# Last output projection with tokens on partitions, its residual turned in squares of 32 during the last layer's attention

## The chip, the cores and the metric

The kernel runs on one core of a Trainium2 chip. The metric is the device time of one execution in microseconds (us): the median over three runs for the kernel before. Beside the timed runs there is one execution taken by the hardware profiler; it has its own time, and its span runs from the first to the last instruction recorded. The core's engines are TensorE (PE in the profile, with its weight loads as PEld), VectorE (DVE), ScalarE (ACT), GpSimd (POOL) and SyncE (SP). Each takes its own instructions in the order in which the program lists them. SP and POOL issue the transfers (DMAs) here; sixteen DMA engines carry them out. The tensors that carry data between stages lie in the chip's memory (DRAM below); tiles lie in the core's own memory, 128 partitions wide.

## What is computed

The input is an image of 48 x 48 tokens with 768 channels. Two layers follow, each a group norm, a multi-head attention with relative positions, and a residual:

```python
def _L1_conv_ref(x, qkv_w, qkv_b, proj_w, proj_b, rel_pos_h, rel_pos_w):
    ...
    qkv = x.reshape(B, N, C) @ qkv_w.T + qkv_b
    ...
    attn = jnp.einsum('bnd,bmd->bnm', q * scale, k)
    ...
    attn = (attn.reshape(B * nh, H, W, H, W) + rel_h[:, :, :, :, None] + rel_w[:, :, :, None, :]).reshape(B * nh, N, N)
    attn = jax.nn.softmax(attn, axis=-1)
    out = jnp.einsum('bnm,bmd->bnd', attn, v)
    ...
    out = out @ proj_w.T + proj_b
    return out
...
x = x + _L0_conv_ref(_gn(x), ...)
x = x + _L1_conv_ref(_gn(x), ...)
return x
```

N is 2304 tokens, C 768 channels, 12 heads of 64 channels. The first layer differs in its weights only (a low-rank addition to q and v). The change concerns the last line of the last layer: `x + (out @ proj_w.T + proj_b)`, with x the residual.

## The kernel before

**Layout.** Through both layers the activations lie with channels on partitions: a block of 384 tokens (QB) is a tile of 128 partitions, 6 channel tiles (CT) and 384 tokens. There are six such blocks (NQB), in three pairs (b, b + 3). The input is turned into this layout at the start by TensorE transposes; the residual of the second layer is kept in DRAM in the same layout (`residuals[1]`, six tensors f_res1_b).

**Stages.** For each layer: group norm, projection to k, v and q with the relative-position terms, attention, output projection. The order of each engine's instructions is set by a scheduler when the program is built, from the order of the source; instructions wrapped in `in_order` keep their order in the source on their engine.

**Attention** (`attend_plain`, L864). It works through 30 blocks: 6 pairs of heads, and for each of them the queries in four blocks of 512 and one of 256. Numbered from 0, blocks 4, 9, 14, 19, 24 and 29 are the short ones. For each block the scores are made in two batches of nine key tiles (ps_sc, three buffers, L967), ScalarE takes the exponential (pt, L981), VectorE adds the pt up (sum, L987) and TensorE multiplies them by the values (ps_ov, L1006); the values of a batch follow the scores of the next. At a block's end the sum is cast in three parts (L996 to L999), TensorE sums it over the keys (ps_d), VectorE takes the reciprocal (L1021) and scales the result (L1025); POOL stores rec and o (L1030, L1032).

What the attention loads comes through SP's queue: the queries and the rel rows of the next block (`fetch_queries`, two q and 24 rel loads; two sets of buffers), and during the last block of a pair of heads the keys and values of the next pair (`keys_of`, L893, and `values_of`, L906; one set of buffers, so that a load waits until the old keys have been read).

After each block from block 1 on, the loop takes one step of the generator `beside` (L1080, L1081):

```python
                if i > 0:
                    next(beside, None)
```

In the kernel before, `beside` (L1249) first loads the projection's weights `w_all` and bias `bt`, and then takes four steps on VectorE that prepare the factors of the seven products.

**Output projection** (`out_project`, L1123). A 2 x 2 block product is made by seven products in place of eight (`seven_products`, L433). For each of the three pairs of token blocks and each of three channel tiles (`co`) there are seven products psy of three matmuls each: weights as the stationary side, 128 output channels on the partitions of the result, 384 tokens along it. ScalarE copies two of the products out (kept_p), VectorE forms the sums and adds them, with the bias, into y, which holds the residual (L1183, L1184). In the last layer y must then be turned to tokens on partitions: 36 TensorE transposes for a pair of blocks (psn, L1200), six copies by ScalarE (L1202) and six stores to the output on SP (L1203). The tiles for the first pair of blocks (y_1_0, y_1_1, oT_1_0, oT_1_1) lie where attention's buffers come free (L1265), and are loaded before the attention ends. `judge` (L1084) looks at all reciprocals and decides whether a second, slower variant of the whole computation must run; it doesn't run with these inputs.

Of the kernel before, what the change touches and what calls it, by code (L numbers as in the profile page):

```python
# [9 lines left out]
F32 = mybir.dt.float32  # L10
# [8 lines left out]
P = 128  # L19
# [52 lines left out]
def compute(ctx: ExitStack, tc: tile.TileContext, x, layers, out, run, bad):  # L72
# [1011 lines left out]
    def judge(ps_j):  # L1084

        cols = NH * N // P
        with tc.tile_pool(name="judge", bufs=1) as jp:
            r = jp.tile([P, 2, cols], F32, tag="r", name="judged")
            low = jp.tile([P, 2, cols], F32, tag="low", name="low")
            good = jp.tile([P, 2], F32, tag="good", name="good")  # L1090
            col = jp.tile([P, 1], F32, tag="col", name="col")
            nc.vector.memset(col, 1.0)
            for li in range(2):
                nc.sync.dma_start(
                    r[:, li, :],
                    recs[li].rearrange("h q -> (h q)").rearrange("(p c) -> p c", p=P),
                )
# [5 lines left out]
            ps = ps_j.tile([P, 1024], F32, tag="n", name="n_good")[0:1, 0:2]  # L1103
# [16 lines left out]
            )  # L1120
            lo += n

    def out_project(ly, li, od, w, bt, first, res, xT, next_res, beside):  # L1123


        last = xT is None
        with ExitStack() as es:
            tp = es.enter_context(tc.tile_pool(name="p3_t", bufs=1, **REUSE))
            kp = es.enter_context(tc.tile_pool(name="p3_k", bufs=2, **REUSE))
            rp = es.enter_context(tc.tile_pool(name="p3_r", bufs=2, **REUSE))  # L1130
            yp = es.enter_context(tc.tile_pool(name="p3_y", bufs=2, **REUSE))
            ps_y = es.enter_context(tc.tile_pool(
                name="ps_y", bufs=4 if last else 8, space=PSUM, **REUSE
            ))
            ps_n = None
            if last:
                op = es.enter_context(tc.tile_pool(name="p3_o", bufs=2 * TPB, **REUSE))
                ps_n = es.enter_context(tc.tile_pool(name="ps_n", bufs=2, space=PSUM, **REUSE))
            for at, b in enumerate((1, 0, 2)):
                pair = (b, b + HB)  # L1140
                if last and not shifted and at == HB - 1:
                    judge(ps_n)
                if not last:
                    y = [xT[i] for i in pair]
                elif at == 0:
                    y = first[2:]
                else:
                    y = yp.tile([P, 2, CT, QB], F32, tag="y", name=f"y_{b}")
                    y = [y[:, i] for i in range(2)]
# [12 lines left out]
                blocks = {  # L1162
                    f"{i + 1}{j + 1}": oT[j][:, i * HP : (i + 1) * HP]
                    for i in range(2) for j in range(2)
                }
                t = tp.tile([P, 4, HP, QB], F32, tag="t", name=f"oT_t_{b}")
                right = sums_of_b(blocks, t)
                for co in range(HP):
                    def product(i):
                        left_of, right_of = FACTORS[i]  # L1170
                        ps = ps_y.tile([P, QB], F32, tag="y", name=f"psy_{b}_{co}_{i}")
                        for t in range(HP):
                            nc.tensor.matmul(  # L1173
                                ps, lhsT=w[left_of][:, t, ts(co, P)], rhs=right[right_of][:, t, :],
                                start=(t == 0), stop=(t == HP - 1),
                            )
                        return ps

                    def result(at, x, more):
                        i, j = int(at[0]) - 1, int(at[1]) - 1  # L1180
                        ch = i * HP + co
                        to = y[j][:, ch, :]
                        nc.vector.tensor_add(to, to, more)  # L1183
                        nc.vector.scalar_tensor_tensor(  # L1184
                            to, x, bt[:, ch : ch + 1], to, ALU.add, ALU.add
                        )
                        if not last:
                            nc.vector.bn_stats(stats[:, ch, pair[j], :], to)
# [4 lines left out]
                for i in range(2):  # L1193
                    if not last:
                        nc.gpsimd.dma_start(next_res[pair[i]], y[i])
                        continue
                    for j in range(TPB):
                        ps = ps_n.tile([P, 1024], F32, tag="n", name=f"psn_{b}_{i}_{j}")
                        for t in range(CT):
                            nc.tensor.transpose(ps[:, ts(t, P)], y[i][:, t, ts(j, P)], ident)  # L1200
                        o = op.tile([P, C], F32, tag="o", name=f"o_{b}_{i}_{j}")
                        nc.scalar.copy(o, ps[:, 0:C])  # L1202
                        nc.sync.dma_start(out[ts(pair[i] * TPB + j, P), :], o)  # L1203

    residuals = [[scratch(f"res{li}_{b}", [P, CT, QB]) for b in range(NQB)] for li in range(2)]
    def begin(li, es):
# [14 lines left out]
    for li, ly in enumerate(layers):  # L1221
# [19 lines left out]
            scratch(f"o{li}_{lo}", [CT, P, min(OB, N - lo)]) for lo in range(0, N, OB)  # L1241
        ]
        with tc.tile_pool(name="p3_w", bufs=1, **REUSE) as p3:
            w_all = p3.tile([P, CT, C], F32, tag="w", name="wproj")
            bt = p3.tile([P, CT], F32, tag="bt", name="bproj")
            s = p3.tile([P, 3, HP, HP * P], F32, tag="s", name="wproj_s")
            w, steps = sums_of_a(matrix_blocks(w_all, HP * P), *(s[:, i] for i in range(3)))
# [12 lines left out]
            if last:  # L1260
                p3_first = es.enter_context(
                    tc.tile_pool(name="p3_first", bufs=1, side="right", **REUSE)
                )

                y_late, *first_out, y_soon = (  # L1265
                    p3_first.tile([P, CT, QB], F32, tag=name, name=name)
                    for name in ("y_1_1", "oT_1_0", "oT_1_1", "y_1_0")
                )
                first_out += [y_soon, y_late]
# [12 lines left out]

            k_steps = prepare()
            out_project(
                ly, li, od, w, bt, first_out, residuals[li], xT,
                None if last else residuals[li + 1], iter(()) if last else k_steps,
            )
            if not last:
# [57 lines left out]
```

## Time and profile before

| what | us |
|---|---|
| median of 3 runs | 3268.39 |
| lowest, highest | 3266.74, 3270.97 |
| the profiled execution | 3271.64 |
| its span | 3269.8 |
| last layer's attention, in the span | about 2107 to 3126 |
| last output projection, in the span | 3126 to 3270 |

The mean TensorE clock granted in the profiled execution is 0.993 of full speed. All times inside the execution below are us from the start of the span. A line of the timeline gives the start, the length, the engine, the source line, the operation, the tiles written and read, their shapes and a count; in brackets stands the idle time before it and what ended that. "SPq" is SP's queue issuing transfers. In a line of groups, the number after the bar is the busy time and the mean in ns of one instruction. In the list of transfers the last number is the median time from issue to landing. In the row of a stretch there is, for each engine, the busy time and the number of instructions, then the clock, the share of the DMA engines' time and GB/s.

Of the last output projection the profile shows 378 records of psy matmuls (two for each of the 189 matmuls), 486 ns each on the average, overlapping in steady work: 12 records in 3.87 us. The 108 transposes take 14.0 us of busy time in all, the 18 copies 801 ns each.

### The profile page before, as it was taken

To read this page: it belongs to the slowest core of one execution; us is meant where nothing else is said; L and a number is where in the kernel's file an instruction comes from. 1 tells how busy PE (TensorE), PEld (TensorE's weight loads), DVE (VectorE), ACT (ScalarE), POOL (GpSimd) and SP (SyncE) were. 2 spreads that over 40 slices of the span, in tenths; PEclk is the share of its full clock that TensorE was granted. 3 is DMA by queue.
4 is the path that set the end of the run, shared out by engine and by line. 5 is a ranking of instruction groups with operands and counts; after the bars stand their busy time and mean duration, and the time that the engine had idled before them with its cause. 6 is when DMAs were issued, how large, how long until landed. Compare 5 with 4: busy or idle time off the path is not lost.

```text
span 3269.8 us, 50021 instructions
## 1 busy us (share of the span) xinstructions
PE 3219.1 (98%) x19708; PEld 2010.7 (61%) x19708; DVE 2098.2 (64%) x2275; ACT 1446.6 (44%) x1655; POOL 374.0 (11%) x701
## 2 busy tenths in 40 slices
PE   8999999999999999999989999999999999999998
PEld 5555666565666565665555566656666665656665
DVE  8432437777777777777775234577777777777764
ACT  3111436555555565553011014555555565656511
POOL 2145110000000000000012531100000000000000
PEclk9999999999999999999999999999999999999999
DMA  7333388353626262634234335865444363525251
GB/s 266 128 85 74 127 263 213 77 131 77 139 68 152 65 154 64 145 71 159 102 121 147 61 105 185 250 151 119 94 115 101 99 120 79 140 75 129 55 196 60
DMA packets 219091, 405.61 MB, mean 124 GB/s; under 512 B 41392, under 2 KB 108880, under 8 KB 215008
## 3 DMA queue, kind: packets, MB, share of 16 engines
q1 hardware_dynamic: 177984, 260.08, 32.4%
q0 software_dynamic: 40864, 142.23, 13.8%
q8 instruction: 159, 2.61, 0.3%
q14 instruction: 84, 0.69, 0.1%
HBM read 253.27 MB, written 148.89 MB: 123 GB/s over the span
## 4 chain that ended last, share of the span: by engine, by line
PE 88%; issue 6%; DVE 2%; DMA 1%; POOL 1%; SPq 1%; ACT 1%; POOLq 0%; DVEq 0%
PE ps_sc L954 34%; PE ps_ov L954 25%; PE ps_v L523 7%; PE psy L1173 7%; PE ps_q L698 6%; PE ps_k L523 4%; PE ps_d L954 1%; PE psr L637 1%; DMA f_r<-relw 1%; POOL f_k L567 1%; PE psc L637 0%; DVE relw L392 0%; PE psn L1200 0%; ACT relw L391 0%; DMA flat<-in_relh_t_dram 0%
## 5 line engine op out<-in xcount | busy, mean ns | idle before, releaser
L987 DVE TENSOR_TENSOR sum<-sum,pt 128x1024 f32<-128x1024 f32 (+1 forms) x960 | 1070.8, 1115 | 188.3 <-ACT pt L981 97.2
L981 ACT ACTIVATE pt<-ps_sc 128x1024 f32<-128x1024 f32 (+1 forms) x1080 | 1011.2, 941 | 192.1 <-PE ps_sc L954 105.8
L954 PE MATMUL ps_sc<-q,k 64*128 64x512 f32 (+1 forms) x8640 | 1086.1, 371 | 1.3 <-DVE relw L392 0.6
L954 PEld LDWEIGHTS ps_sc<-q,k 64*128 64x128 f32 x8640 | 786.6, 186 | 208.1 <-issue 43.9
L954 PE MATMUL ps_ov<-pt,v 128*64 128x512 f32 (+1 forms) x4320 | 857.7, 551 | 0.0
L954 PEld LDWEIGHTS ps_ov<-pt,v 128*64 128x64 f32 x4320 | 301.1, 137 | 497.6 <-issue 443.0
L954 PE MATMUL ps_sc<-rel,places 64*128 64x512 f32 (+1 forms) x2160 | 415.3, 371 | 2.9 <-DMA rel<-f_r 2.9
L698 PE MATMUL ps_q<-xT,w_q 128*128 128x384 f32 x864 | 285.7, 489 | 0.6 <-DVE v L587 0.6
L1032 POOL DMA_DIRECT2D f_rec<-rec x120 | 58.3, 490 | 1776.6 <-DVE rec L1021 1776.4
L1026 ACT ACTIVATE o<-o,v_bias 128x512 f32<-128x512 f32 (+1 forms) x60 | 40.9, 682 | 449.5 <-DVE o L1025 449.5
L954 PEld LDWEIGHTS ps_sc<-rel,places 64*128 64x128 f32 x2160 | 213.3, 185 | 33.2 <-DMA rel<-f_r 2.9
L698 PEld LDWEIGHTS ps_q<-xT,w_q 128*128 128x128 f32 x864 | 163.4, 191 | 110.3 <-issue 2.9
L1021 DVE RECIPROCAL rec<-ps_d 128x512 f32<-128x512 f32 (+1 forms) x60 | 181.8, 3030 | 2.5 <-PE ps_d L954 2.5
L987 DVE TENSOR_TENSOR sum<-pt 128x1024 f32<-128x1024 f32 (+1 forms) x60 | 67.1, 1119 | 140.2 <-ACT pt L981 140.2
L601 POOL DMA_DIRECT2D f_v<-v x288 | 137.3, 485 | 105.8 <-DVE v L587 94.4
L704 DVE TENSOR_SCALAR x_q<-ps_q,bt 128x384 f32<-128x384 f32 x72 | 44.3, 617 | 160.0 <-PE ps_q L698 160.0
L523 PE MATMUL ps_k<-xt,w_k 128*128 128x384 f32 x432 | 143.4, 488 | 3.5 <-DVE xt L427 2.6
L996 ACT CAST sum<-sum 128x1024 bf16<-128x1024 f32 (+1 forms) x60 | 57.6, 960 | 167.7 <-DVE sum L987 167.7
L523 PE MATMUL ps_k<-xT,w_k 128*128 128x384 f32 x324 | 116.4, 513 | 4.7 <-DVE xT L249 4.6
L523 PEld LDWEIGHTS ps_k<-xt,w_k 128*128 128x128 f32 x432 | 81.6, 190 | 62.9 <-PE ps_k L523 3.0
L999 DVE TENSOR_TENSOR sum<-sum,sum 128x1024 bf16<-128x1024 f32 (+1 forms) x60 | 67.1, 1119 | 61.6 <-ACT sum L998 61.6
L997 DVE TENSOR_TENSOR sum<-sum,sum 128x1024 f32<-128x1024 f32 (+1 forms) x60 | 67.1, 1118 | 61.5 <-ACT sum L996 61.5
(172 smaller groups left out, 2383.4 us busy)
## 6 DMA issues: line engine op xcount, KB each, us to landing
rel<-f_r SPq DMA_DIRECT2D x1152, 96.0 KB, 4.3
f_k<-xs POOLq DMA_DIRECT2D x72, 384.0 KB, 2.9
f_q<-xs_q POOLq DMA_DIRECT2D x48, 576.0 KB, 3.8
k<-f_k SPq DMA_DIRECT2D x48, 576.0 KB, 4.9
q<-f_q SPq DMA_DIRECT2D x96, 256.0 KB, 3.3
f_r<-relh POOLq DMA_DIRECT2D x48, 432.0 KB, 5.0
f_r<-relw POOLq DMA_DIRECT2D x8, 2592.0 KB, 18.2
f_v<-v POOLq DMA_DIRECT2D x288, 48.0 KB, 2.0
```

The lines of the kernel that those rows point to most:

```text
L523: nc.tensor.matmul(ps, lhsT=x, rhs=y, start=(t == 0), stop=(t == HP - 1))
L601: nc.gpsimd.dma_start(vd[to : to + KG, :], v[ts(r, KG), k])
L698: nc.tensor.matmul(ps, lhsT=w[:, t, ts(pr, P)], rhs=xT[b][:, t, :], start=(t == 0), stop=(t == CT - 1),)
L954: in_order(nc.tensor.matmul(*args, **kwargs))
L981: nc.scalar.activation(pt, ps[:, :, 0 : self.n], AF.Exp)
L987: nc.vector.tensor_add(self.sum, self.first if kt == 1 else self.sum, pt)
L996: nc.scalar.copy(hi, self.sum)
L997: nc.vector.tensor_sub(self.sum, self.sum, hi)
L999: nc.vector.tensor_sub(lo, self.sum, mid)
L1021: nc.vector.reciprocal(self.rec, ps)
L1032: nc.gpsimd.dma_start(recs[li][2 * self.pair + r : 2 * self.pair + r + 1, to], self.rec[r * HD : r * HD + 1, :],)
L1173: nc.tensor.matmul(ps, lhsT=w[left_of][:, t, ts(co, P)], rhs=right[right_of][:, t, :], start=(t == 0), stop=(t == HP - 1),)
```

## The change

In the last layer's output projection the two sides of each matmul change places: the attention's output is the stationary side, 128 tokens at a time, and the weights' factors stream through, 384 channels. The result has tokens on partitions, as the output wants it, so the transposes and the copies behind them are gone, and the sums are stored straight from y. The residual must then also lie with tokens on partitions, and carry the bias, which is no longer one number per partition.

That is done by the new generator `turn`, run in the steps of `beside` during the last layer's attention, for each of the six blocks of 384 tokens: load the block of the residual, add the bias in six activations on ScalarE, transpose it in squares of 32 by one VectorE instruction over 128 x 2304 elements, and store it in 24 transfers on POOL, each of 32 partitions by 12 runs of 32 numbers, to `res_tokens` in DRAM, tokens by channels. The tile `both` holds a block and its transposed form; it has one buffer, with the tag "w" that the projection's weights use after it. The output projection loads its y from `res_tokens`.

```diff
-    def out_project(ly, li, od, w, bt, first, res, xT, next_res, beside):
+    def out_project(li, od, w, bt, first, res, xT, next_res, beside):
...
-            yp = es.enter_context(tc.tile_pool(name="p3_y", bufs=2, **REUSE))
+            yp = es.enter_context(tc.tile_pool(name="p3_y", bufs=2 * TPB, **REUSE))
             ps_y = es.enter_context(tc.tile_pool(
-                name="ps_y", bufs=4 if last else 8, space=PSUM, **REUSE
+                name="ps_y", bufs=7 if last else 8, space=PSUM, **REUSE
             ))
...
-                for i in range(2):
-                    nc.sync.dma_start(y[i], res[pair[i]])
+                if last:
+                    def tokens(x, j):
+                        return x.rearrange("(k b j p) c -> b j p k c", k=2, b=HB, j=TPB)[b, j]
+
+                    for j in range(TPB):
+                        nc.sync.dma_start(y[j], tokens(res, j))
...
-                for co in range(HP):
+                for part in range(HP):
...
+                            x, y = w[left_of][:, t], right[right_of][:, t]
+                            if last:
+                                x, y = y[:, ts(part, P)], x
+                            else:
+                                x = x[:, ts(part, P)]
                             nc.tensor.matmul(
-                                ps, lhsT=w[left_of][:, t, ts(co, P)], rhs=right[right_of][:, t, :],
-                                start=(t == 0), stop=(t == HP - 1),
+                                ps, lhsT=x, rhs=y, start=(t == 0), stop=(t == HP - 1)
                             )
...
+                        if last:
+                            to = y[part][:, j, ts(i, HP * P)]
+                            nc.vector.tensor_add(to, to, more)
+                            nc.vector.tensor_add(to, to, x)
+                            return
...
                     seven_products(kp, QB, product, result)
+                    if last:
+                        for k in (1, 0):
+                            nc.sync.dma_start(tokens(out, part)[:, k], y[part][:, k])
...
-                    for j in range(TPB):
-                        ps = ps_n.tile([P, 1024], F32, tag="n", name=f"psn_{b}_{i}_{j}")
-                        for t in range(CT):
-                            nc.tensor.transpose(ps[:, ts(t, P)], y[i][:, t, ts(j, P)], ident)
-                        o = op.tile([P, C], F32, tag="o", name=f"o_{b}_{i}_{j}")
-                        nc.scalar.copy(o, ps[:, 0:C])
-                        nc.sync.dma_start(out[ts(pair[i] * TPB + j, P), :], o)
+    def turn(res, to, pool, bt):
+        for b in range(NQB):
+            both = pool.tile([P, 2, CT, QB], F32, tag="w", name=f"x_turned_{b}")
+            x, turned = both[:, 0], both[:, 1]
+            in_order(nc.sync.dma_start(x, res[b]))
+            yield
+            for t in range(CT):
+                in_order(nc.scalar.activation(
+                    x[:, t], x[:, t], AF.Identity, bias=bt[:, t : t + 1]
+                ))
+                if t == HP - 1:
+                    yield
+            in_order(nc.vector.transpose(
+                turned.rearrange("p t q -> p (t q)"), x.rearrange("p t q -> p (t q)")
+            ))
+            rows = to[ts(b, QB), :].rearrange("(f i) c -> i f c", i=32)
+            for t in range(CT):
+                for r in range(P // 32):
+                    lo = t * P + r * 32
+                    in_order(nc.gpsimd.dma_start(
+                        rows[:, :, lo : lo + 32],
+                        turned[ts(r, 32), t].rearrange("p (f j) -> p f j", j=32),
+                    ))
...
-            def beside(w_all=w_all, bt=bt, steps=steps, ly=ly):
+            def beside(li=li, ly=ly, p3=p3, bt=bt, w=w):
+                in_order(nc.sync.dma_start(bt, ly.proj_bt))
+                if li == 1:
+                    yield from turn(residuals[1], res_tokens, p3, bt)
+                w_all = p3.tile([P, CT, C], F32, tag="w", name="wproj")
+                s = p3.tile([P, 3, HP, HP * P], F32, tag="s", name="wproj_s")
                 in_order(nc.sync.dma_start(w_all, ly.proj_w.rearrange("(t p) n -> p t n", p=P)))
-                in_order(nc.sync.dma_start(bt, ly.proj_bt))
+                factors, steps = sums_of_a(
+                    matrix_blocks(w_all, HP * P), *(s[:, i] for i in range(3))
+                )
+                w.update(factors)
                 yield
                 yield from steps
```

The tiles of the first pair of blocks are laid out anew for y's new shape (y_1_0, y_1_1, y_1_2, each 128 tokens of both blocks by 768 channels; as much memory in all as before), and judge's one matmul gets a small accumulator of its own in place of a buffer of the transposes.

More of the change, by code (lines that the diff above doesn't have):

```diff
@@ L1102, in judge @@
                 )
-            ps = ps_j.tile([P, 1024], F32, tag="n", name="n_good")[0:1, 0:2]
+            ps = ps_j.tile([P, 2], F32, tag="n", name="n_good")[0:1]
             nc.tensor.matmul(ps, lhsT=col, rhs=good, start=True, stop=True)
@@ L1130, in out_project @@
             rp = es.enter_context(tc.tile_pool(name="p3_r", bufs=2, **REUSE))
-            yp = es.enter_context(tc.tile_pool(name="p3_y", bufs=2, **REUSE))
+            yp = es.enter_context(tc.tile_pool(name="p3_y", bufs=2 * TPB, **REUSE))
             ps_y = es.enter_context(tc.tile_pool(
-                name="ps_y", bufs=4 if last else 8, space=PSUM, **REUSE
+                name="ps_y", bufs=7 if last else 8, space=PSUM, **REUSE
             ))
-            ps_n = None
+            ps_j = None
             if last:
-                op = es.enter_context(tc.tile_pool(name="p3_o", bufs=2 * TPB, **REUSE))
-                ps_n = es.enter_context(tc.tile_pool(name="ps_n", bufs=2, space=PSUM, **REUSE))
+                ps_j = es.enter_context(tc.tile_pool(name="ps_j", bufs=1, space=PSUM, **REUSE))
             for at, b in enumerate((1, 0, 2)):
@@ L1141, in out_project @@
                 if last and not shifted and at == HB - 1:
-                    judge(ps_n)
+                    judge(ps_j)
                 if not last:
@@ L1147, in out_project @@
                 else:
-                    y = yp.tile([P, 2, CT, QB], F32, tag="y", name=f"y_{b}")
-                    y = [y[:, i] for i in range(2)]
+                    y = [
+                        yp.tile([P, 2, C], F32, tag="y", name=f"y_{b}_{j}") for j in range(TPB)
+                    ]
                 if at == 0:
@@ L1156, in out_project @@
                     fetch_output(oT[i], od, pair[i])
-                for i in range(2):
-                    nc.sync.dma_start(y[i], res[pair[i]])
+                if last:
[4 more added lines that the diff above has]
+                else:
+                    for i in range(2):
+                        nc.sync.dma_start(y[i], res[pair[i]])
                 if at == 0:
@@ L1167, in out_project @@
                 right = sums_of_b(blocks, t)
-                for co in range(HP):
+                for part in range(HP):
                     def product(i):
                         left_of, right_of = FACTORS[i]
-                        ps = ps_y.tile([P, QB], F32, tag="y", name=f"psy_{b}_{co}_{i}")
+                        ps = ps_y.tile([P, QB], F32, tag="y", name=f"psy_{b}_{part}_{i}")
                         for t in range(HP):
+                            x, y = w[left_of][:, t], right[right_of][:, t]
+                            if last:
+                                x, y = y[:, ts(part, P)], x
+                            else:
+                                x = x[:, ts(part, P)]
                             nc.tensor.matmul(
-                                ps, lhsT=w[left_of][:, t, ts(co, P)], rhs=right[right_of][:, t, :],
-                                start=(t == 0), stop=(t == HP - 1),
+                                ps, lhsT=x, rhs=y, start=(t == 0), stop=(t == HP - 1)
                             )
@@ L1180, in result @@
                         i, j = int(at[0]) - 1, int(at[1]) - 1
-                        ch = i * HP + co
+                        if last:
[3 more added lines that the diff above has]
+                            return
+                        ch = i * HP + part
                         to = y[j][:, ch, :]
@@ L1186, in result @@
                         )
-                        if not last:
-                            nc.vector.bn_stats(stats[:, ch, pair[j], :], to)
+                        nc.vector.bn_stats(stats[:, ch, pair[j], :], to)
                     seven_products(kp, QB, product, result)
+                    if last:
+                        for k in (1, 0):
+                            nc.sync.dma_start(tokens(out, part)[:, k], y[part][:, k])
                 for _ in beside:
                     pass
-                for i in range(2):
-                    if not last:
+                if not last:
+                    for i in range(2):
@@ L1195, in out_project @@
                         nc.gpsimd.dma_start(next_res[pair[i]], y[i])
-                        continue
-                    for j in range(TPB):
-                        ps = ps_n.tile([P, 1024], F32, tag="n", name=f"psn_{b}_{i}_{j}")
-                        for t in range(CT):
-                            nc.tensor.transpose(ps[:, ts(t, P)], y[i][:, t, ts(j, P)], ident)
-                        o = op.tile([P, C], F32, tag="o", name=f"o_{b}_{i}_{j}")
-                        nc.scalar.copy(o, ps[:, 0:C])
-                        nc.sync.dma_start(out[ts(pair[i] * TPB + j, P), :], o)
+    def turn(res, to, pool, bt):
[21 more added lines that the diff above has]
+                    ))
@@ L1205, in compute @@
     residuals = [[scratch(f"res{li}_{b}", [P, CT, QB]) for b in range(NQB)] for li in range(2)]
+    res_tokens = scratch("res_tokens", [N, C])
     def begin(li, es):
@@ L1243, in compute @@
         with tc.tile_pool(name="p3_w", bufs=1, **REUSE) as p3:
-            w_all = p3.tile([P, CT, C], F32, tag="w", name="wproj")
             bt = p3.tile([P, CT], F32, tag="bt", name="bproj")
-            s = p3.tile([P, 3, HP, HP * P], F32, tag="s", name="wproj_s")
-            w, steps = sums_of_a(matrix_blocks(w_all, HP * P), *(s[:, i] for i in range(3)))
-            def beside(w_all=w_all, bt=bt, steps=steps, ly=ly):
+            w = {}
+            def beside(li=li, ly=ly, p3=p3, bt=bt, w=w):
[4 more added lines that the diff above has]
+                s = p3.tile([P, 3, HP, HP * P], F32, tag="s", name="wproj_s")
                 in_order(nc.sync.dma_start(w_all, ly.proj_w.rearrange("(t p) n -> p t n", p=P)))
-                in_order(nc.sync.dma_start(bt, ly.proj_bt))
+                factors, steps = sums_of_a(
+                    matrix_blocks(w_all, HP * P), *(s[:, i] for i in range(3))
+                )
+                w.update(factors)
                 yield
@@ L1263, in compute @@
                 )
-                y_late, *first_out, y_soon = (
-                    p3_first.tile([P, CT, QB], F32, tag=name, name=name)
-                    for name in ("y_1_1", "oT_1_0", "oT_1_1", "y_1_0")
+                y_2, y_1, *first_out, y_0 = (
+                    p3_first.tile(shape, F32, tag=name, name=name)
+                    for name, shape in (
+                        ("y_1_2", [P, 2, C]), ("y_1_1", [P, 2, C]), ("oT_1_0", [P, CT, QB]),
+                        ("oT_1_1", [P, CT, QB]), ("y_1_0", [P, 2, C]),
+                    )
                 )
-                first_out += [y_soon, y_late]
+                first_out += [y_0, y_1, y_2]
             else:
@@ L1284, in compute @@
             out_project(
-                ly, li, od, w, bt, first_out, residuals[li], xT,
+                li, od, w, bt, first_out, res_tokens if last else residuals[li], xT,
                 None if last else residuals[li + 1], iter(()) if last else k_steps,
```

## The prediction

> **What bounds the kernel now.** I read the page's busy table first, then the busy time by stretches, then the last layer's attention and the end of the span in order of time.
>
> ```profile
> PE 3219.1 (98%) x19708; PEld 2010.7 (61%) x19708; DVE 2098.2 (64%) x2275; ACT 1446.6 (44%) x1655; POOL 374.0 (11%) x701
> ...
> core 0: us, PE busy (x) PEld busy (x) DVE busy (x) ACT busy (x) POOL busy (x), PEclk, DMA share, GB/s
> 2107.00:3126.00 1019.00, 1017.60 (x7735) 638.56 (x7732) 745.24 (x636) 583.08 (x631) 45.98 (x89) 1.00 0.47 110
> ```
>
> TensorE is busy 98% of the span. The second row is the last layer's attention, 2107 to 3126 us: TensorE works 1017.6 of 1019.0 us there, VectorE 745 (73%), ScalarE 583 (57%). So nothing added on the last two engines costs time unless TensorE is made to wait; the same holds for a queue.
>
> TensorE waits if keys are late. The keys of the next pair of heads have one set of buffers (L896), so they are fetched in the last block of a pair. The first such change in this layer, SP's queue and then TensorE:
>
> ```profile
> 2254.60 1.01 SPq L946 DMA_DIRECT2D rel<-f_r  x1
> 2255.71 13.92 SPq L899 DMA_DIRECT2D k<-f_k  x4
> 2273.24 0.37 SPq L908 DMA_DIRECT2D v<-f_v  x1
> ...
> 2269.09 4.11 PE L954 MATMUL ps_ov<-pt,v 128*64 128x256 f32 x36
> 2273.12 1.19 PE L954 MATMUL ps_sc<-q,k 64*128 64x512 f32 x8
> ```
>
> SP takes its instructions in order. It issues the first two key loads at 2255.7, once the old keys are read (the row's 13.92 us reach to the last two, which wait for the second half). A key load lands 4.9 us after issue, at 2260.6, and the first score of the next pair starts at 2273.12: 12.5 us in hand.
>
> The end of the span:
>
> ```profile
> 3256.82 0.61 DVE L1184 SCALAR_TENSOR_TENSOR y<-psy,bproj,y 128x384 f32<-128x384 f32 x1
> 3257.48 0.20 PEld L1200 LDWEIGHTS psn<-ident,y 128*128 128x128 f32 x2 [0.42 <-DVE y L1184]
> 3257.85 1.50 ACT L1202 COPY o<-psn 128x768 f32<-128x768 f32 x2 [6.89 <-PE psn L1200]
> ...
> 3260.46 1.58 PE L1200 MATMUL psn<-ident,y 128*128 128x128 f32 x12 [0.19 <-ACT o L1202]
> 3261.37 1.50 ACT L1202 COPY o<-psn 128x768 f32<-128x768 f32 x2 [0.26 <-PE psn L1200]
> ```
>
> VectorE has the last sum at 3257.43; 36 transposes and six copies follow, and the last copy ends at 3262.87. Only then can the last store go.
>
> **What is removed.** 108 transposes (psn, L1200) and 18 copies (L1202). In the steady stretch 12 matmul records of psy take 3.87 us. After the first group of blocks TensorE needs 7.81 us from the first transpose (weights at 3166.25) to the first record of the third product (3174.06); the 12 psy records among them are worth 3.87, so the transposes cost 3.94. After the second, 3210.83 to 3218.96: 8.13 - 3.87 - 0.12 for judge's matmul, which stays, = 4.14. At the end 3262.87 - 3257.43 = 5.44. **Sum 13.5 us off the path.** The swapped operands leave 189 products of 128x128 by 128x384; the value products (ps_v, L523) run that way round already at 486 ns a record, and psy's records take 486. I cost the swap at nothing. The bias add in place (scalar_tensor_tensor, 615 ns) becomes an add (555 ns), 36 times: 2.2 us of an engine with idle time here. Stores now leave per 128 tokens and not after a whole group: 384 KB each, as before. Seven product buffers for four only help.
>
> **What is moved into the last attention.** For each of six blocks of 384 tokens: one load of 1152 KB on SP, six activations of 128x384, one VectorE transpose of 128x2304, 24 stores on POOL of 48 KB, each 384 runs of 128 bytes; 6, 36, 6 and 144 in all. `next(beside)` is called once after each block from the second on, and two calls make one block of x: block 1 loads x 0, block 2 does three activations, block 3 the other three, the transpose, the 24 stores, **and the load of x 1, which goes into the same buffer and so waits until all 24 stores have landed**. That pattern repeats every second block; after block 13 the projection's weights take the buffer the same way.
>
> The wait stands in SP's queue. Behind it stands what SP issues next. In the changed program's instruction order these are: for x 1, twelve rel loads and then the keys of pair 1; for the weights, eight rel loads and then the keys of pair 3. Blocks 3 and 13 are both followed by the short last block of a pair (256 queries). For x 2 to x 5 the waits fall into long blocks and only queries and rel rows needed a block later stand behind.
>
> Durations for the first, in the clock of this trace (block 3's sums end at about 2250):
>
> ```profile
> 2247.78 1.04 ACT L998 CAST sum<-sum 128x1024 bf16<-128x1024 f32 x1 [1.29 <-DVE sum L997]
> 2249.95 5.40 ACT L981 ACTIVATE pt<-ps_sc 128x512 f32<-128x512 f32 x9 [1.14 <-PE ps_sc L954]
> ...
> 2250.00 1.35 DVE L412 TENSOR_TENSOR wproj_s<-wproj_s,wproj 128x1152 f32<-128x1152 f32 x1
> ...
> L1026 ACT ACTIVATE o<-o,v_bias 128x512 f32<-128x512 f32 (+1 forms) x60 | 40.9, 682 | 449.5 <-DVE o L1025 449.5
> ...
> L630 POOL DMA_DIRECT2D f_q<-xs_q x48 | 34.6, 723 | 203.3 <-ACT xs_q L386 176.2 <-DVE xs_q L387 17.0 <-ACT columns L714 10.1
> L601 POOL DMA_DIRECT2D f_v<-v x288 | 137.3, 485 | 105.8 <-DVE v L587 94.4
> f_v<-v POOLq DMA_DIRECT2D x288, 48.0 KB, 2.0
> ```
>
> - Three activations: between 0.510 (128x256, same line) and 0.725 us (128x512), so 0.62 each, 1.85 us from the end of the cast at 2248.82: 2250.7. The next block's exponentials start 0.7 us later than 2249.95; three score buffers of 1.15 us each hide that.
> - The transpose has no row. The 128x1152 add above takes 1.35 us, so 128x2304 takes 2.7 at the same rate; bounds 1.35 (twice that rate) and 5.4 (half of it). I take 2.7: 2253.4. VectorE's own delay is hidden: it idles 2.4 us before 2263.
> - The stores: POOL's time per store runs from 0.485 us (16 rows, f_v) to 0.723 (384 rows, f_q, the same number of pieces). I take 0.723: 24 x 0.723 = 17.4; bounds 11.6 and, with the 0.88 us of the 768-piece fu load, 21. The last lands 2.0 us later (f_v; bounds 1.5 and 5). **SP goes on at 2253.4 + 17.4 + 2.0 = 2272.8**, where it was at 2248 before.
> - Then x 1 (0.4 us), twelve rel loads at 0.62 us each as in this stretch (2252.75, 2253.36, ...): 7.4, and the keys at 2280.6. They land 4.9 us later, 2285.5, or 2.9 later still if the 1152 KB ahead of them move at some 400 GB/s, as the key loads do in the DMA row of this stretch. I take 2286. TensorE wanted them at 2273.1: **13 us of standing still.** With the low bounds (transpose 1.35, stores 11.6, landing 1.5) SP goes on at 2265.2 and the keys land at 2278: 5. With the high ones, 2282.2 and 2298: 25.
> - The weights after block 13: eight rel loads (5.0) but 2304 KB ahead of the keys (5.8 at 400 GB/s): keys at 2272.8 + 0.4 + 5.0 + 5.8 + 4.9 = 2288.9 in the same clock, 2283.1 if the weights don't hold them up. I take 2287: **14 us** (bounds 2 and 25, by the same ends).
> - For x 2 to x 5, SP goes on about 23 us into a block of 37.5 and x lands 9.9 us after (the y load of the same size): 33. ScalarE meets x at the block's end, so 4 us are left, and I cost these at nothing. With the high bounds x lands at 43 and each costs 3 us after the buffers: 12 in all.
>
> The rest of POOL's queue, the f_rec and f_o stores behind the 24, is up to 9 us late; its readers come blocks later.
>
> Do 128-byte rows go slower than the queue issues them? The f_rec stores are such rows:
>
> ```profile
> q0 software_dynamic: 64, 0.00, 1.6%
> f_rec<-rec POOLq DMA_DIRECT2D x2, 2.0 KB, 1.5
> ```
>
> Those are 2.5 us in which two stores ran: 64 packets, 1.6% of 16 x 2.5 us, 10 ns each. At 10 ns the 24 packets that one store gives each DMA engine take 0.24 us, a third of the 0.72 of their issue. [...] The f_v row above (one every 0.485 us, each 2.0 us to landing) shows that stores overlap; what thousands of short writes cost together, no row here shows.
>
> **Sum.** -13.5 + 13 + 14 = +13.5 us on the profiled execution (3271.6 us, of which 3269.8 are span): 3285. Against the median of the runs, 3268.4, which is 3.2 lower: **3282 us**, slower by 0.4%.
>
> **Rivals.** About 0.2% (6.5 us) is what this kernel's runs can tell from no change.
> 1. *The wait is covered: faster.* Place: SP's queue after blocks 3 and 13. Price 0 for 27: 3255 us. Keys come in time if SP goes on by 2260, that is if the 24 stores are out within 5 us, 0.2 us each; it decides for "faster" from two stalls below 3.5 us each. For it: the 10 ns packets. Against it: no POOL store in the page takes under 0.485 us. 15%, with 3255 to 3262.
> 2. *Gain and stalls cancel.* Near the low bounds: two stalls of 5, so 3268.4 - 13.5 + 10 = 3265. For it: only 32 partitions a store, nearer f_v's 16. 20%, 3262 to 3275.
> 3. *Short writes are slow.* At 1.5 us a store the 24 take 36, each of the two stalls grows by 19, and x 2 to x 5 land after their block's end by some 14 us, of which 10 each reach TensorE: 3268.4 + 13.5 + 38 + 40 = 3360. For it: all the small rows in the trace are few at a time. 15%, from 3300 up.
> 4. *My sum*, 50%, own range 3275 to 3300.
>
> So faster 0.15, same 0.20, slower 0.65. The range reaches into rival 1 and the lower part of rival 3: 3257 to 3312, leaving out about 0.2.
>
> **What will show it.** Right: in the changed profile TensorE stands idle 10 to 15 us before the first score of the second and of the fourth pair of the last layer, released by a key load; POOL shows 144 stores of about 0.7 us; the projection has no gap between groups and is 13 us shorter. Wrong: key loads issued within a few us of before; stores near 0.2 us (rival 1) or POOL waiting for its own earlier stores (rival 3); ScalarE waiting for x at long blocks' ends; or a projection with waits of its own, for y or for a store.

## The result, and the profile after

| kernel | median us | lowest, highest | against before, 95% interval |
|---|---|---|---|
| before | 3268.07 (5 runs) | 3266.24, 3270.97 | |
| changed | 3286.53 (5 runs) | 3284.80, 3287.59 | 1.0056 [1.0041, 1.0071] |

The change costs 18.5 us. The profiled execution took 3286.01 us, of which 3284.0 are span.

Two differences of times in the two traces say where it went. From the first scores of the last layer's attention to the first product of the projection: 2105.95 to 3125.84 before, 2101.91 to 3152.03 after, so 1019.9 and 1050.1: **the attention is 30.2 us longer**. From there to the end of the span: 144.0 and 132.0: **the projection is 12.0 us shorter**. (The attention began 4.0 us earlier in the execution after, in stages that the change doesn't touch. So a moment of the trace after corresponds to one 4.0 us later in the trace before.)

The page after, lines that answer to those shown of before:

```profile
PE 3209.8 (98%) x19600; PEld 1993.1 (61%) x19600; DVE 2111.7 (64%) x2281; ACT 1450.6 (44%) x1673; POOL 462.0 (14%) x845
...
q0 software_dynamic: 45472, 149.32, 15.2%
...
L954 PE MATMUL ps_sc<-q,k 64*128 64x512 f32 (+1 forms) x8640 | 1087.1, 371 | 25.2 <-issue 11.8
```

TensorE has 9.3 us less work and is still 98% busy. The last row is the one to look at: before its scores TensorE now stands idle for 25.2 us in all, where the page of before gives that group 1.3 us:

```profile
L954 PE MATMUL ps_sc<-q,k 64*128 64x512 f32 (+1 forms) x8640 | 1086.1, 371 | 1.3 <-DVE relw L392 0.6
```

The place is found in order of time. POOL, SP and TensorE at the first change of pairs (stores, loads, scores; the second line is what SP waited for before the load of x 1: us in all, times, longest):

```profile
2249.23 14.61 POOL L1238 DMA_DIRECT2D f_res_tokens<-x_turned  x24 [19.87 <-DVE x_turned L1231]
...
SPq L1223 <- DMA f_res_tokens<-x_turned: 22.2, 2, 17.4
...
2266.04 0.34 SPq L1223 DMA_DIRECT2D x_turned<-f_res  x1
...
2275.08 0.98 SPq L899 DMA_DIRECT2D k<-f_k  x2
...
2265.51 4.11 PE L954 MATMUL ps_ov<-pt,v 128*64 128x256 f32 x36
2280.81 1.22 PE L954 MATMUL ps_sc<-q,k 64*128 64x512 f32 x4 [11.19 <-DMA k<-f_k]
```

The 24 stores go out one behind the other until 2263.8. SP issues nothing from 2243.5 to 2266.0, when they have landed; then x 1, twelve rel loads, and the keys at 2275.1. TensorE has been idle since 2269.6 and goes on when they are there. The weights do the same after block 13 (SP's queue, then TensorE):

```profile
2600.07 0.42 SPq L946 DMA_DIRECT2D rel<-f_r  x1
2622.12 0.40 SPq L1293 DMA_DIRECT2D wproj<-in_proj_w_dram  x1
...
2631.68 1.91 SPq L899 DMA_DIRECT2D k<-f_k  x4
...
2636.02 1.22 PE L954 MATMUL ps_sc<-q,k 64*128 64x512 f32 x4 [11.79 <-issue]
```

The trace names no releaser for this stall ("issue"); the keys issued from 2631.68 on landed 4.3 to 7.2 us later, and 4.3 us is when TensorE goes on.

Idle time is not the whole price. The granted clock (the number after the five engines) by stretches: before the stall, behind each of the two stalls, and further on:

```profile
2230.00:2245.00 15.00, 15.00 (x102) 8.33 (x98) 11.95 (x11) 10.13 (x11) 0.00 (x0) 1.00 0.51 121
2280.80:2287.00 6.20, 5.98 (x30) 4.28 (x32) 0.00 (x0) 1.90 (x2) 0.00 (x0) 0.56 1.07 365
2287.00:2298.50 11.50, 11.50 (x106) 9.20 (x102) 10.69 (x9) 7.35 (x8) 0.15 (x1) 1.00 1.03 212
2636.00:2642.00 6.00, 5.81 (x28) 4.23 (x30) 0.00 (x0) 1.73 (x2) 0.00 (x0) 0.56 1.07 368
```

In the 6 us behind each idle stretch TensorE has 0.56 of its clock on the mean, which costs 0.44 x 6.2 + 0.44 x 6.0 = 5.4 us. So of the 30.2 us, 23.4 are idle time (11.19 + 0.22 and 11.79 + 0.16), 5.4 slow clock, and 1.4 are left (the kernel `later` below, which has neither, keeps 1.3 of them). Behind the first stall the clock was 0.50 from 2280.8 to 2286.0; full speed came back 5.4 us after the scores had begun again there, and 5.2 us behind the second.

### The profile page after: what moved, and what is told of

Same layout as the page of the kernel before. It is cut to its first block, busy times and chain, and to the rows that moved or that the text cites. A ratio compares the mean times of both kernels' runs of the same rounds, so it can differ in the third digit from the quotient of the medians.

```text
span 3284.0 us, 50036 instructions
## 1 busy us (share of the span) xinstructions
PE 3209.8 (98%) x19600; PEld 1993.1 (61%) x19600; DVE 2111.7 (64%) x2281; ACT 1450.6 (44%) x1673; POOL 462.0 (14%) x845
## 3 DMA queue, kind: packets, MB, share of 16 engines
q0 software_dynamic: 45472, 149.32, 15.2%
## 4 chain that ended last, share of the span: by engine, by line
PE 89%; issue 3%; DVE 3%; DMA 2%; ACT 1%; POOL 1%; SPq 1%; DVEq 0%; POOLq 0%; ACTq 0%
PE ps_sc L954 34%; PE ps_ov L954 24%; PE ps_q L698 9%; PE ps_v L523 7%; PE psy L1186 7%; PE ps_k L523 4%; PE psr L637 1%; PE ps_d L954 1%; DVE sum L987 1%; PE psc L637 1%; DMA rel<-f_r 1%; DVE relw L392 1%; POOL f_k L567 1%; ACT pt L981 1%; ACT relw L391 0%
## 5 line engine op out<-in xcount | busy, mean ns | idle before, releaser
L954 PE MATMUL ps_sc<-q,k 64*128 64x512 f32 (+1 forms) x8640 | 1087.1, 371 | 25.2 <-issue 11.8
```

The costliest lines, as they stand in the source:

```text
L954: in_order(nc.tensor.matmul(*args, **kwargs))
```

## The experiments

The kernel before was run beside each group of kernels; the ratio and its interval are against those runs.

| kernel | median us | ratio to before, 95% interval |
|---|---|---|
| proj (projection alone) | 3253.89 | 0.9959 [0.9945, 0.9973] |
| turn (turning alone) | 3300.90 | 1.0102 [1.0086, 1.0117] |
| later | 3256.10 | 0.9964 [0.9952, 0.9977] |
| later_w | 3270.59 | 1.0008 [0.9999, 1.0017] |
| pool | 3272.76 | 1.0015 [1.0006, 1.0024] |
| split | 3270.17 | 1.0008 [0.9999, 1.0017] |
| quarters | 3270.15 | 1.0008 [0.9999, 1.0017] |
| double | 3305.10 | 1.0113 [1.0098, 1.0129] |
| early | 3265.16 | 0.9987 [0.9978, 0.9996] |
| early_s | 3257.23 | 0.9963 [0.9949, 0.9977] |

### The two halves: projection alone, turning alone

```diff
 proj:
-                    yield from turn(residuals[1], res_tokens, p3, bt)
-                li, od, w, bt, first_out, res_tokens if last else residuals[li], xT,
+                li, od, w, bt, first_out, x if last else residuals[li], xT,
```

> The turned copy is not made; the last projection, tokens on partitions, reads the kernel's input x in place of the residual, and the bias of that layer is left out. This is the projection's edit alone. Theory: the stage is 12.0 us shorter by the two traces (144.0 to 132.0), and the attention is that of the kernel before: 3268 - 12 = about 3256. If the stage's gain came from something that the copy in the attention brings (weights spread later, other addresses), the time is nearer 3268. If the projection alone gains the 13.5 us forecast, 3254.6.

This kernel leaves out the bias and reads the input x in place of the residual, so it doesn't compute the function and serves for its time alone. Measured: 3253.9 beside 3267.4, 13.5 us less. Its attention is the one of before, 1019.3 us long (2101.12 to 3120.46), and the stage after it 130.4.

The second kernel is the one before with `turn` and its call put in.

> The turning of x alone, with the projection as it was before: the copy in token order is made during the attention and nothing reads it. Theory: the attention grows as in the changed kernel, by 30.2 us in the two traces (1019.9 to 1050.1 from its first products to the projection's), and the projection stays: 3267.4 + 30.2 = about 3298. With the projection alone at 3253.9 the two parts then add up to the change: 3298 - 13.5 = 3284 against 3286.5. If the stall needs the projection's other room in memory or its other weights, 3268 to 3280.

Measured: 3300.9 beside 3268.3, 32.6 us more. The sum of the halves is -13.5 + 32.6 = +19.1, beside +18.5 for the change: they add up, and the loss lies in the turning alone.

### The same work one block later

```diff
 later, at the end of each block in turn:
+            yield
 later_w, in its place:
+            if b < NQB - 1:
+                yield
```

> Each load that waits for the 24 stores of the block before it is issued one block of the attention later: the loads of x stand after blocks 1, 4, 7, 10, 13 and 16, the weights after block 19, each behind the keys' loads. All work of the change stays. Theory (the time lost in the attention is SP's queue: the keys of a pair stand behind a load that waits for stores): both idle stretches of TensorE go, 14.3 and 15.6 us of shift by the two traces, the 12.0 us won in the projection stay: 3286.5 - 29.9 = about 3257, under the kernel before. Rival (contention: the 36 activations, 6 transposes, 144 stores and 13 loads slow the attention wherever they stand): no less than 3280. A result between, near 3271, would say that only one of the two stretches was the queue.

> As the kernel with every load one block later, but the load of the weights is not put off: the loads of x stand after blocks 1, 4, 7, 10, 13 and 16, and the weights after block 18, ahead of the keys of the pair that starts at block 20, with 24 stores still to land. One wait of the two is left, and it stands at another pair's end than in the changed kernel. Theory (queue): 3257 + 15.6 = about 3272, with one idle stretch of some 11 us in front of a pair's first products, the granted clock near 0.56 for the 6 us after it. Rival (contention): the same time as with the weights later, whichever that is.

Measured: 3256.1 and 3270.6, both within 2 us of the theory. With every load behind the keys, TensorE's idle time before these scores is 1.3 us in the whole stretch from 2095 to 3130, and the attention takes 1021.2 us (2099.50 to 3120.69), 1.3 more than before. TensorE by the row of this stretch:

```profile
L954 PE MATMUL ps_sc<-q,k 64*128 64x512 f32 (+1 forms) x4320 | 540.7, 370 | 1.3 <-DVE relw L392 0.8
```

That is all that 36 activations, 6 transposes, 144 stores and 7 loads cost when nothing waits behind them; contention falls as a cause, for the work moved by one block (the last kernel below leaves it in the changed kernel's blocks). With the weights alone left in front of keys, one stall is back, at another pair's end:

```profile
2791.33 1.22 PE L954 MATMUL ps_sc<-q,k 64*128 64x512 f32 x4 [9.85 <-issue]
```

The stall follows the load, not the pair. `later` beats both the kernel before and the changed one.

### The loads on POOL's queue: the wait moves on

```diff
-            in_order(nc.sync.dma_start(x, res[b]))
+            in_order(nc.gpsimd.dma_start(x, res[b]))
...
-                in_order(nc.sync.dma_start(w_all, ly.proj_w.rearrange("(t p) n -> p t n", p=P)))
+                in_order((nc.gpsimd if li == 1 else nc.sync).dma_start(w_all, ly.proj_w.rearrange("(t p) n -> p t n", p=P)))
```

> The loads of x and, in the second layer, the load of the projection's weights are issued from POOL's queue, where the 24 stores stand that they wait for; nothing of theirs stands in SP's queue, the blocks are those of the changed kernel. Theory (queue): the keys never stand behind a wait: about 3257. POOL carries the stores of rec and of the attention's outputs too, which may now wait the 2 us that a store takes to land; if these are late for SP's loads of them, some us come back. Rival (contention): 3286, since all transfers are made at the same blocks as in the changed kernel.

Measured: 3272.8, neither the theory's 3257 nor the rival's 3286. (Its runs lie between 3266.9 and 3276.9; the trace is of the shortest, and what the longer ones add is not shown.) The keys are issued from 2247.6 on and nobody waits for them. TensorE still stands still in the same two places. POOL, ScalarE and TensorE at the first, VectorE at the second:

```profile
2263.95 0.57 POOL L1223 DMA_DIRECT2D x_turned<-f_res  x1 [0.45 <-issue]
...
2271.23 1.62 ACT L1226 ACTIVATE x_turned<-x_turned,bproj 128x384 f32<-128x384 f32 x3 [3.72 <-DMA x_turned<-f_res]
...
2273.81 2.07 PE L954 MATMUL ps_sc<-q,k 64*128 64x512 f32 x8 [3.63 <-ACT pt L981]
...
2622.36 1.36 DVE L412 TENSOR_TENSOR wproj_s<-wproj 128x1152 f32<-128x1152 f32 x1 [7.96 <-DMA wproj<-in_proj_w_dram]
```

x 1 itself is late. Its activations stand in ScalarE's program order at the end of the short block; the exponentials behind them wait, the three score buffers fill, TensorE stops. The weights do it through VectorE: the sums of pt stand behind the first sum of the weights, ScalarE gets no free pt, TensorE is idle for 6.4 us. In the changed kernel the first of these waits was 1.77 us long and hidden, since TensorE stood waiting for keys anyway. The theory was right about the cause and wrong about the cure: the wait had a second and a third way to TensorE.

### Room of its own for the turned copy

```diff
-            x, turned = both[:, 0], both[:, 1]
+            x = both[:, 0]
...
+            s = pool.tile([P, 3, HP, HP * P], F32, tag="s", name=f"turned_{b}")
+            turned = s[:, 0:2].rearrange("p i t q -> p (i t) q")
```

> The turned copy of a block of x gets room of its own (the room in which the sums of the weights are made later), so that the buffer of x is free as soon as VectorE has turned it. All loads, stores, activations and transposes stand at the changed kernel's places in every queue; the loads of x 1 to x 5 and of the weights wait for the transpose and no longer for the 24 stores. Theory (what the change loses is the wait for the landed stores, which the keys stand behind in SP's queue): both stretches go, and since x and the weights land some 20 us earlier, ScalarE and VectorE don't wait for them either: about 3256, as with the loads one block later. If TensorE's idle time came back with the blocks of the changed kernel, the place of the work and not the wait would be the cause: 3272 (as from POOL's queue) to 3286.

Measured: 3270.2, not 3256. The expectation's sentence that everything stands at the changed kernel's places in every queue was not true of the kernel: the scheduler put the load of x 1 at another place in SP's queue, ahead of the queries and all 24 rel loads of the next block. What SP waited for in this stretch, and what it then issued:

```profile
SPq L1223 <- DVE turned L1233: 37.2, 1, 37.2
...
2247.48 0.34 SPq L1223 DMA_DIRECT2D x_turned<-f_res  x1
...
2266.69 1.86 SPq L899 DMA_DIRECT2D k<-f_k  x4
```

SP stood 37.2 us before the load of x 1, now for VectorE's transpose, and the keys come after 26 more loads, at 2266.7: earlier than the changed kernel's 2275.1, later than the 2255.7 of before. TensorE was idle for 3.2 and 5.6 us, with the slow clock behind both. So this run doesn't decide what it was made for. It does show that SP's queue can make the stall without any wait for stores in it: the wait is for VectorE, and the two boundaries still cost 14 us (3270.2 beside 3256.1 for `later`).

On top of it, storing each quarter of a result as it is ready:

```diff
                             nc.vector.tensor_add(to, to, x)
+                            nc.sync.dma_start(tokens(out, part)[:, j, ts(i, HP * P)], to)
                             return
...
-                        for k in (1, 0):
-                            nc.sync.dma_start(tokens(out, part)[:, k], y[part][:, k])
```

> As the kernel with the turned copy in its own room, and each quarter of a token tile's result (128x384) is stored as soon as it is added, 36 stores in place of 18. In the changed kernel the last two stores, 384 KB each, are issued at the very end and land a median 3.3 us later. Theory: the last store is a quarter of 192 KB, the others have gone before: 1 to 2 us less than the kernel it is made from, 3254 to 3255. If more stores on SP's queue delay a load of the stage, or the end hangs on something else than the size of the last stores, the same 3256 or some us more.

Measured: 3270.15 beside 3270.17 for the kernel it is made from. From the projection's first product to the end of the span it takes 129.9 us (3136.37 to 3266.3) where the other takes 130.4: half a microsecond at most. Smaller last stores don't shorten the end by the 1 to 2 us expected; half a microsecond is less than the 1.5 us by which the endings of the other kernels differ (below).

### Twice as many stores

```diff
-            for t in range(CT):
+            for to_t in range(2 * CT):
+                t, to_i = to_t % CT, (to, twice)[to_t // CT]
```

> Each of the 24 stores of a block is made twice, the second time into a tensor that nothing reads; 48 stores per block. Theory (queue): a load goes on when the last of the 48 has landed, 24 x 0.617 = 14.8 us later than in the changed kernel; both waits in front of keys grow by that, the longer idle time costs no further slow stretch: 3286.5 + 29.6 = 3316, and more if the loads of q and rel in the long blocks are now late too (up to four more waits of 15 us). Rival (the stall hangs on transfers or on the number of waits and not on POOL's issuing): about 3290.

Measured: 3305.1, about halfway between the rival's 3290 and the theory's 3316. POOL, SP and TensorE at the first change of pairs:

```profile
2262.96 14.58 POOL L1239 DMA_DIRECT2D f_res_twice<-x_turned  x24
...
2279.20 0.34 SPq L1223 DMA_DIRECT2D x_turned<-f_res  x1
2279.63 2.22 SPq L899 DMA_DIRECT2D k<-f_k  x4
...
2286.78 2.45 PE L954 MATMUL ps_sc<-q,k 64*128 64x512 f32 x8 [19.09 <-DMA k<-f_k]
```

SP goes on 31.8 us after the first store (2247.44 to 2279.20), where it was 16.8 in the changed kernel: +15.0, as 24 stores more should make it. TensorE's idle time grew by 7.9 only, because here the rel loads were put ahead of the wait and the keys come 0.4 us after it instead of 9.0. The weights now stand behind the keys of pair 3, and their lateness reaches TensorE through VectorE (14.1 us idle) as from POOL's queue; x 4 costs 8.0 more through ScalarE. The queue's wait is as long as the theory has it; what it costs depends on what the scheduler places behind it.

### Early loads, then the last wait

```diff
 early, in turn (load(b) issues the load of x b on nc.gpsimd, then() that of the weights; room as in split):
-            in_order(nc.sync.dma_start(x, res[b]))
+            x = x_next
...
             in_order(nc.vector.transpose(
...
+            if b < NQB - 1:
+                x_next = load(b + 1)
+            else:
+                then()
             rows = to[ts(b, QB), :].rearrange("(f i) c -> i f c", i=32)
 early_s, in beside, behind the weights' factors:
                 yield
+                if li == 1:
+                    yield
```

> As the kernel with the turned copy in its own room, but the loads of x and of the second layer's weights are issued from POOL's queue, right behind the transpose that frees their buffer and ahead of that block's 24 stores; SP carries none of them. Blocks, activations, transposes and stores stay where the changed kernel has them. Two waits are taken away at once: the one in front of the keys (SP) and the one for x 1 and the weights on ScalarE and VectorE, which were 3.7 and 8.0 us long when these loads stood behind the stores in POOL's queue. Theory (these two waits are all that the attention loses, whatever the block): x 1 lands some 6 us after 2247 and the weights some 10 us after 2595, both ahead of their use near 2267 and 2619; no idle stretch at either place, 3256 as with every load one block later. Rival (the short blocks hold too little slack for the turning itself, so that the place of the work costs): about 3270, as from POOL's queue behind the stores and from SP's with own room.

Measured: 3265.2. The first boundary runs without any idle time. The second has 5.9 us left; VectorE and TensorE there:

```profile
2621.26 1.36 DVE L412 TENSOR_TENSOR wproj_s<-wproj 128x1152 f32<-128x1152 f32 x1 [7.45 <-DMA f_rec<-rec]
...
2636.31 2.07 PE L954 MATMUL ps_sc<-q,k 64*128 64x512 f32 x8 [5.88 <-ACT pt L981]
```

The trace names a store of rec as the last to end. That store was issued at 2616.4 and landed 6.3 us later, when the sum had already begun, so by these times it is not what the sum waited for. What the sum needs is its room, which is the room that I had given to the turned copy: the last of that block's 24 stores was issued at 2615.2 and landed 6.0 us later, at 2621.2, just before the sum. These stores were late because POOL had stood 6.9 us, up to 2604.5, until the load of the weights ahead of them had landed. The next kernel takes the sum out of that wait:

> The kernel with own room and early loads from POOL, and the first sum of the weights (128x1152 on VectorE) one block later. In that kernel the first boundary of pairs has no idle TensorE any more; at the second, the sum stood in VectorE's queue 7.5 us, until 2621.3, since its room was the one that the last block's turned copy was still being stored from, ScalarE's next tiles waited behind the sums of pt, and TensorE was idle for 5.9 us before 2636.3. Theory (a third queue, VectorE's, with a wait for stores in it): the sum starts after the stores have landed and waits for nothing; no idle stretch is left at either boundary, 3265.2 - 9 = about 3256, as with every load one block later. Rival (the short block itself lacks the slack for what it carries): the idle time at 2636 stays, 3265, or moves to another place.

Measured: 3257.2. From 2105 to 3130 TensorE's longest idle stretch before scores is 0.74 us, and the attention takes 1020.6 us (2105.72 to 3126.36):

```profile
L954 PE MATMUL ps_sc<-q,k 64*128 64x512 f32 (+1 forms) x4320 | 541.0, 370 | 1.6 <-DVE relw L392 0.7 <-ACT pt L981 0.4
```

With all three waits away and all of the turning left in the changed kernel's blocks (only the sums of the weights stand one block later), the loss is gone; the place of the turning in the short blocks is not a cause.

## Why the prediction was right

3282 us were forecast, 3286.5 measured; slower was given 0.65. The mechanism, its two places and its order of size are what the trace and the runs show. That the number came so near is in part luck, since errors cancel: the two stalls were forecast at 27 us of idle time and took 23.4, which is 3.6 less; the slow clock behind them (5.4), a smaller gain in the projection (1.5) and the 1.4 us left in the attention add 8.3. Step by step:

- **Projection, -13.5.** The projection alone gains 13.5. In the changed kernel's profile it is 12.0: the last add to the end of the span takes 7.9 us there (3276.06 to 3284.0) and 6.4 in the projection alone (3244.49 to 3250.9), behind the same two last stores. All ten kernels with this projection take 124.0 us from the first product to the last add. The ending behind it takes 6.4 us in `proj`, `pool`, `split`, `early` and `early_s`, and 7.7 to 8.1 in the changed kernel, `later`, `later_w` and `double`, with the same two last stores; since `later` has no stall, the stalls don't make the difference. What does was not tried further.
- **Stores, 0.723 us each:** 0.617 on the mean, 14.61 for 24. This made the forecast 2.8 us late, and SP's going on with it: 2272.8 forecast, 2266.0 + 4.0 = 2270.0 measured in the same clock.
- **Transpose, 2.7 us** (bounds 1.35 and 5.4): 2.58. **Activations, 0.62:** 0.605. **Landing of a store, 2.0:** 2.0, median.
- **Keys 7.8 us behind SP's going on:** 9.0, since one rel load had to wait for some 3 us. They landed 5.7 us after their issue; 5.4 was forecast.
- **The stalls, 13 and 14 us:** idle 11.4 and 12.0. The mis-sized term is here, and it is one that the sum didn't have: the price of an idle stretch is the idle time and the slow clock behind it, 11.4 + 2.7 and 12.0 + 2.6. I read the granted clock for the stretches before and didn't ask what it would be after a stall.
- **x 2 to x 5 at nothing:** right. TensorE has no idle stretch above 0.4 us there. ScalarE waited 1.8 us for x 1 and for no other.
- **Rival 1, covered:** no; it needed stores of 0.2 us each, and they took 0.617. **Rival 2, cancel:** no; the stalls were near my values and not near their low bounds.
- **Rival 3, short writes are slow:** no. Each block's 24 stores end as fast as they are issued: one every 0.617 us, and each lands a median 2.0 us later (4.1 at the most). In the stretch from 2249 to 2266, where little but these stores runs, the 16 DMA engines were busy half of the time (the last number): `q0 software_dynamic: 891, 1.45, 50.3%`. On queue q0 the packets rose from 40864 to 45472, 32 for each of the 144 stores, while a store has 384 runs of 128 bytes and I had reckoned a packet for each: many runs go in one packet.

What I didn't see was how little the cure is worth that the theory suggests, another queue for the load that waits. My bounds for x 2 to x 5 treated the second way, through ScalarE, and it was there at x 1 too, hidden behind the first.

## What to carry to other kernels

In these runs a load that waited for its buffer held up everything behind it in its queue (in the changed kernel SP issued nothing for 22.5 us, in `split` it stood 37.2 us): before moving work under another stage, look at what stands behind each new wait in SP's, POOL's, ScalarE's and VectorE's program order, and at which of it is due first. Moving the wait to another queue was no cure here, since what was loaded was itself late (`pool`, 3272.8 beside 3256.1 for `later`); moving the work by one block, where the next due thing is far, took one line and turned +18.5 us into -11.3. The nine idle stretches of TensorE behind which the granted clock was read, 3.2 to 19.1 us long, all had 0.50 of the clock behind them, and such a stretch has to be priced with it.

## What was not expected of the hardware

The slow clock follows short stalls too. Behind idle times of 3.6 (pool), 5.6 (split), 5.9 (early), 13.3 (turn) and 19.1 us (double) the next 2 us ran at 0.50 each time, and by the means of the rows full speed came back 3.4, 5.7, 3.6, 4.0 and 5.9 us later, without a clear relation to the length of the idle time. The longest slow stretch even followed the shortest stall: behind 3.2 us of idle time in `split` (2268.1 to 2271.3) the first 0.7 us still had the full clock by the mean of its row, 0.67 over 2 us, and at least the next 6.0 us, up to 2278.0, had half of it. The first of the five, idle, then in steps of about 2 us:

```profile
2270.20:2273.80 3.60, 0.00 (x0) 0.00 (x0) 0.00 (x0) 2.57 (x5) 0.00 (x0) 0.99 1.07 338
2273.80:2275.80 2.00, 1.99 (x10) 1.59 (x12) 1.09 (x1) 1.79 (x2) 0.00 (x0) 0.50 1.03 182
2275.80:2277.80 2.00, 2.00 (x16) 1.57 (x14) 1.68 (x3) 1.03 (x1) 0.00 (x0) 0.66 0.33 80
2277.80:2280.00 2.20, 2.20 (x22) 1.86 (x20) 1.82 (x2) 1.85 (x2) 0.00 (x0) 1.00 0.69 189
```

Here 3.63 us of idle time cost 1.0 + 0.7 = 1.7 us more in clock, nearly half as much again.
